# One order for five engines, written by a clock: a state-space and mixture-of-experts layer on Trainium2

## The chip, the cores and the metric

The kernel runs on one core of one Trainium2 chip. A core has TensorE (PE; its weight loads are shown as PEld), VectorE (DVE), ScalarE (ACT), GpSimd (POOL) and SyncE (SP), which here issues every DMA transfer. Each engine takes its instructions strictly in the order in which they are written, and waits for the others by semaphores. The metric is the time of one execution on the device in microseconds (us): 2043.07 is the median of three runs before the change, which lie between 2033.55 and 2044.17.

## The reference

The input is u, 4 sequences of 2048 tokens of 256 numbers, all in float32. The layer has two halves, each with a residual:

```python
x = x + ssm(layernorm(x));   x = x + moe(layernorm(x))
# ssm: x, z = split(u @ W_in.T + b_in);  delta, B, C from x @ W_x.T + b_x
#   delta = softplus(delta_raw @ W_dt.T + b_dt);  A = -exp(A_log)        # 512 x 16
#   for each token: h = h * exp(delta * A) + x * delta * B;  y = sum_n(h * C)
#   (y + x * D) * silu(z) @ W_out.T + b_out
# moe: 4 experts, softmax router, top 2, weights w (not renormalized)
#   h_e = relu(x @ Wi.T + lora_e);  out = sum_e w_e * (h_e @ Wo.T)       # 1024 wide
```

The mean and variance of a layernorm are taken over the 256 numbers of a token; eps is 1e-5.

## The kernel before

**Tiling.** The tokens are cut into 16 chunks of 512 (`TC`), four to a sequence. Inside a chunk the channels lie on the 128 partitions in four blocks (`d`), and time runs along the free axis, so that one `tensor_tensor_scan` on VectorE carries one of the 16 states `n` of one block through 512 tokens. There are 64 scans in a chunk, 1024 in all (the list `states`).

**One state.** `decay(i)` on ScalarE writes exp(delta * A) into one of three PSUM buffers dA. `enter(i)` on GpSimd multiplies delta * x by B for two states at once (dBx). `scan(i)` on VectorE joins the two. `read(i)` multiplies by C: on VectorE into hC, or, for 5 of 16 states (`SHARED`), on GpSimd into hP, in which case the scan writes hS. `sum_y(i)` on TensorE adds the result to y by four transposes. `keep(i)` on ScalarE copies the last column as the carry of the next chunk. B and C are broadcast from DRAM by SyncE (`load_bc`). A decay has to wait until the read three states earlier has freed its buffer.

**Around the states.** `front(c)` makes chunk c's inputs: layernorm, its transpose to xnT, the projections `p_in`, delta with softplus, and the gate with silu. `close_y` copies y, turns it back and gates it; `tail(c)` makes the output projection `po` and adds it to u; `ffn(c)` holds the second layernorm, the router (`p_route` to `mask`) and eight half-tiles k of the expert layer: `p_low` (LoRA of the second-best expert, then the difference to the best one), `p_base`, relu, transpose `p_hT`, copy `a_hT`, and, once for two half-tiles, the down projection `p_down` (pf) with its `add`. The relu of each of the two experts is a ScalarE ACTIVATE with the expert's weight as scale (`a_relu`), and both results are transposed into the same PSUM tile. Only the last chunk (`late`) adds the second relu on VectorE (`d_relu`) and transposes once; it then scales by the best expert's weight in `add`.

**LayerNorm.** `layernorm_T` takes the statistics of four 128-token tiles on VectorE (`bn_stats`, `bn_aggr`), 1/sqrt on GpSimd in four small operations (`rstd`), and applies them with four ScalarE ACTIVATEs (`norm`).

**What sets the order.** Every operation goes through `InOrder`, which fixes each engine's order as the program order. A main loop writes the scans i = 0 to 1023 in turn, with the decay two and dBx four states ahead and `sum_y` two or three states behind. All other work is cut into `Step`s with a rough cost. `Pacer.fill` is called twice for each state and puts in the steps that a rough clock calls ready: for VectorE only with a margin of 0.5 us behind their inputs and for at most 0.8 us at a time (`fits`, `ready`). `force` writes what a deadline asks for. Work that does not fit waits, and `begin(c)`, called when chunk c - 1 closes, adds the next chunk's steps behind it. Three PSUM banks ("mm") are shared by all these steps. The order on every engine is fixed when the program is built.

## Time and profile before

| what | value |
|---|---|
| median of 3 runs | 2043.07 us (2033.55 to 2044.17) |
| profiled execution | span 2037.5 us from its first to its last instruction; the page gives no other total |
| busy VectorE / GpSimd / TensorE / ScalarE | 1818.6 / 1779.0 / 1820.4 / 1424.0 us |
| TENSOR_TENSOR_SCAN, all kinds | 1024, from 31.04 us on |
| mean granted TensorE clock | 0.950 |
| ACT_TABLE_LOAD | 64, 82.1 us |

The page gives, for each engine, the busy time and the number of instructions, then the busy share in 40 equal slices, the chain that ended last, and groups of instructions: line, engine, operation, tile written <- tiles read, shape, count, busy us, mean ns of one, and the idle time before them with what ended it. All operations here go through line 30, the recording helper, so groups are told apart by their tiles: plg is the router, pz the expert pre-activations, h the relu output, phT its transpose, pf the down projection, st and mv the layernorm statistics. Durations of successive instructions on an engine overlap a little; TensorE's ends are modelled.

### The profile page before, as it was taken

The numbers are of one execution on the slowest core, as the hardware profiler recorded it, in microseconds if no ns is written. First come the engines' busy times: TensorE is split into PE (matmuls) and PEld (weight loads), VectorE is DVE, ScalarE is ACT, GpSimd is POOL, SyncE is SP. The second block draws the span as 40 slices with busy tenths as digits, with TensorE's granted clock in tenths as the row PEclk, the third lists the DMA queues.
The fourth block names the chain that finished last, engine by engine and source line by source line (L and its number), as shares of the span: only waits on it lengthen the run. The fifth ranks groups of instructions, "written<-read, shape, count | busy, mean of one in ns | idle before, by whom it ended". The sixth has DMA issues, their size and how long they took to land.

```text
span 2037.5 us, 28634 instructions
## 1 busy us (share of the span) xinstructions
PE 1820.4 (89%) x9472; PEld 1251.9 (61%) x9472; DVE 1818.6 (89%) x2370; ACT 1424.0 (70%) x2890; POOL 1779.0 (87%) x1148
## 2 busy tenths in 40 slices
PE   7577798797998998999889899999999898998899
PEld 4445476566666675766557575666756566575655
DVE  3999999899999999999989899899999999899811
ACT  4677777676777768777686777677696877766432
POOL 4999999898999998999998998899999998999600
PEclk8688899798999999999999999999999999998999
DMA  7444445344445453454535344354544544454200
GB/s 237 151 163 157 143 148 171 130 157 164 158 145 166 149 171 137 159 176 144 182 129 175 133 166 149 126 168 141 178 152 160 164 147 158 135 175 145 74 0 21
DMA packets 106132, 300.70 MB, mean 148 GB/s; under 512 B 12864, under 2 KB 39104, under 8 KB 105984
## 3 DMA queue, kind: packets, MB, share of 16 engines
q1 hardware_dynamic: 105984, 298.88, 43.9%
q8 instruction: 74, 1.21, 0.2%
q14 instruction: 74, 0.61, 0.1%
HBM read 289.41 MB, written 9.44 MB: 147 GB/s over the span
## 4 chain that ended last, share of the span: by engine, by line
PE 29%; DVE 14%; ACT 10%; issue 4%; POOL 1%; DMA 0%; DVEq 0%; POOLq 0%; ACTq 0%
PE pz L30 10%; PE y L30 6%; DVE dA L30 6%; PE pf L30 5%; ACT dA L30 4%; PE pin L30 3%; DVE hS L30 3%; DVE hC L30 3%; PE phT L30 2%; ACT L30 1%; ACT delta L30 1%; ACT g L30 1%; PE po L30 1%; DVE u L30 1%; POOL dBx L30 1%
## 5 line engine op out<-in xcount | busy, mean ns | idle before, releaser
L30 POOL TENSOR_TENSOR dBx<-xdt,B 128x1024 f32<-128x1024 f32 x512 | 1205.7, 2363 | 60.4 <-DVE dA L30 20.6
L30 ACT ACTIVATE dA<-delta,a_sb 128x512 f32<-128x512 f32 x1024 | 708.5, 694 | 144.7 <-DVE hC L30 89.6
L30 DVE TENSOR_TENSOR_SCAN dA<-dA,carry,dBx 128x512 f32<-128x512 f32 x528 | 661.1, 1277 | 38.7 <-ACT dA L30 28.2
L30 DVE TENSOR_TENSOR hC<-dA,C 128x512 f32<-128x512 f32 x704 | 470.8, 669 | 0.0
L30 PE MATMUL y<-ident,hC 128*128 128x128 f32 x2816 | 431.8, 284 | 24.4 <-DVE hC L30 24.3
L30 POOL TENSOR_TENSOR hP<-hS,C 128x512 f32<-128x512 f32 x320 | 408.1, 1275 | 2.8 <-PE y L30 2.4
L30 PEld LDWEIGHTS y<-ident,hC 128*128 128x128 f32 x2816 | 344.2, 147 | 105.3 <-DVE hC L30 39.7
L30 DVE TENSOR_TENSOR_SCAN hS<-dA,carry,dBx 128x512 f32<-128x512 f32 x240 | 305.2, 1272 | 22.3 <-ACT dA L30 17.3
L30 PE MATMUL pin<-xnT,w_in_sb 128*128 128x512 f32 x512 | 252.0, 620 | 23.2 <-ACT dbc L30 5.3
L30 PE MATMUL pz<-wi_sb,x2T 128*128 128x512 f32 x512 | 266.1, 645 | 0.0
L30 PEld LDWEIGHTS y<-ident,hP 128*128 128x128 f32 x1280 | 159.7, 147 | 163.9 <-issue 79.8
L30 ACT COPY carry<-dA 128x1 f32<-128x1 f32 x528 | 82.9, 157 | 241.5 <-DVE hC L30 240.3
L30 PE MATMUL y<-ident,hP 128*128 128x128 f32 x1280 | 205.9, 286 | 50.4 <-POOL hP L30 50.2
L30 PE MATMUL pf<-wo_sb,hT 128*128 128x256 f32 x1024 | 238.6, 381 | 6.8 <-ACT hT L30 3.9
L30 DVE TENSOR_TENSOR_SCAN dA<-dA,dBx 128x512 f32<-128x512 f32 x176 | 209.6, 1219 | 14.8 <-ACT dA L30 11.8
L30 ACT ACTIVATE h<-pz,topv 128x512 f32<-128x512 f32 x248 | 167.1, 679 | 77.4 <-PE pz L30 76.6
L30 PEld LDWEIGHTS pf<-wo_sb,hT 128*128 128x128 f32 x1024 | 187.3, 190 | 35.1 <-ACT hT L30 5.2
L30 PE MATMUL pz<-bm_sb,lowT 16*128 16x512 f32 x512 | 167.7, 650 | 23.8 <-ACT delta L30 6.9
L30 PEld LDWEIGHTS pz<-wi_sb,x2T 128*128 128x128 f32 x512 | 93.0, 202 | 121.0 <-issue 121.0
L30 PEld LDWEIGHTS pin<-xnT,w_in_sb 128*128 128x128 f32 x512 | 92.7, 198 | 116.5 <-issue 80.1
L30 PE MATMUL phT<-ident,h 128*128 128x128 f32 x992 | 132.2, 275 | 6.0 <-ACT delta L30 3.1
L30 PEld LDWEIGHTS phT<-ident,h 128*128 128x128 f32 x992 | 114.6, 142 | 31.3 <-issue 17.4
(99 smaller groups left out, 1786.6 us busy)
## 6 DMA issues: line engine op xcount, KB each, us to landing
B<-bc SPq DMA_DIRECT2D x256, 512.0 KB, 3.7
C<-bc SPq DMA_DIRECT2D x256, 512.0 KB, 3.8
ua<-in_u_dram SPq DMA_DIRECT2D x16, 512.0 KB, 5.3
u<-in_u_dram SPq DMA_DIRECT2D x16, 512.0 KB, 5.4
out_dram<-u SPq DMA_DIRECT2D x16, 512.0 KB, 4.8
w_in_sb<-in_w_inT_dram SPq DMA_DIRECT2D x2, 512.0 KB, 4.7
wi_sb<-in_wiT_dram SPq DMA_DIRECT2D x1, 1024.0 KB, 7.2
wo_sb<-in_woT_dram SPq DMA_DIRECT2D x1, 1024.0 KB, 10.6
```

The source lines that it names most:

```text
L30: return self._tc.keep_in_program_order(f(*args, **kwargs))
```

## The change

The order is no longer written by a loop with fillers. All work, scans and decays too, is made of `Step`s with an occupancy, a tail (time until the result is seen) and a due time, counted in states. `Clock.run` takes, over all five engines, the step that can start first; among those of one engine that could start within `SOON` of each other, the one that is due first. `start` counts data, bank and buffer waits; every buffer's release is given as a dependency. TensorE is written down as 1.095 times slower than its full-rate times (`FAST`). A `veto` keeps other ScalarE work from delaying the next decay, until it is overdue. Chunk c - 1's router is due 14 to 30 states, its expert layer 30 to 80 states after chunk c begins. ACT_TABLE_LOADs are counted in the clock.

Beside this: layernorm's mean and sum of squared deviations are taken by two ScalarE ACTIVATEs per tile with a running sum (`mean`, `spread`), into one junk tile, and `rstd` has three operations; every chunk now does what only the last one did: the second expert's relu, scaled by rho (the second-best expert's exponential), is written by ScalarE, the best expert's relu is added to it on VectorE, there is one set of transposes, and `add` scales by `top0` = 1 / sum of exponentials; the router keeps unnormalized exponentials, whose sum comes from the exponential itself, and saves a sum, a multiplication and a copy on VectorE. SHARED, buffer numbers and the three banks are as before.

```diff
-class Pacer:
-    LATENCY = 0.2
-    MARGIN = 0.5
-    LONG = 1.0
-    MOST = 0.8
-    BEGIN = {"pe": 0.7, "act": 0.6, "pool": 0.5, "sp": 0.0}
-    END = {"pe": 2.2, "act": 1.5, "pool": 2.5, "sp": 99.0}
...
-    def fits(self, x, begin):
...
-    def ready(self, x):
...
+    TAIL = {"pe": 0.18, "act": 0.11, "dve": 0.1, "pool": 0.055, "sp": 4.0}
...
+    WAKE = {"pe": 0.055, "act": 0.037, "dve": 0.06, "pool": 0.08, "sp": 0.1}
+    SOON = {"pe": 0.05, "act": 0.02, "dve": 0.02, "pool": 0.05, "sp": 0.05}
+    TABLE = 1.294
...
+    def start(self, x):
+        t = self.free[x.engine]
+        w = self.WAKE[x.engine]
+        for y in x.after:
+            if y.done is None:
+                return None
+            if y.done + w > t:
+                t = y.done + w
+        if x.locks and self.locked:
+            return None
+        if x.takes:
+            if len(x.takes) > sum(b is not None for b in self.bank):
+                return None
+            t = max(t, sorted(b for b in self.bank if b is not None)[len(x.takes) - 1] + w)
+        return t
+    def write(self, x, t):
+        for k in x.takes:
+            k.at = min((b, n) for n, b in enumerate(self.bank) if b is not None)[1]
+            self.bank[k.at] = None
+        x.begin = t
+        self.free[x.engine] = t + self.occ(x)
+        x.done = self.free[x.engine] + x.tail
+        if x.table:
+            self.table = x.table
+        for k in x.gives:
+            self.bank[k.at] = x.done
+        self.locked = (self.locked or x.locks) and not x.unlocks
+        if x.emit:
+            x.emit()
+        if x.then:
+            x.then()
+    def choose(self, engine):
+        seen = []
+        for thread in self.threads:
+            q = thread.of.get(engine)
+            if q:
+                t = self.start(q[-1])
+                if t is not None:
+                    seen.append((t, q[-1], thread))
+        if not seen:
+            return None
+        if self.strict:
+            seen = [s for s in seen if not self.veto(s[1], s[0])]
+            if not seen:
+                return None
+        soon = min(s[0] for s in seen) + self.SOON[engine]
+        return min((s for s in seen if s[0] <= soon), key=lambda s: (s[1].due, s[0]))
+    def run(self):
+        while self.threads:
+            picks = [p for p in map(self.choose, self.free) if p]
+            if not picks:
+                self.strict = False
+                picks = [p for p in map(self.choose, self.free) if p]
+                self.strict = True
+            assert picks, "nothing can be written"
+            t, x, thread = min(picks, key=lambda p: p[0])
+            thread.of[x.engine].pop()
+            thread.left -= 1
+            if not thread.left:
+                self.threads.remove(thread)
+            self.write(x, t)
...
-        def stats(j):
-            if j == 0:
-                q["mv"] = small.tile([P, NJ, 2], F32, tag=f"mv{name[0]}", name=f"mv_{name}")
-            x = small.tile([P, 6], F32, tag="st", name=f"st_{name}_{j}")
-            dve.bn_stats(x, src()[:, j, :])
-            dve.bn_aggr(q["mv"][:, j, :], x)
+        def mean(j):
+            if j == 0:
+                q["nm"] = small.tile([P, NJ], F32, tag=f"nm{name[0]}", name=f"nm_{name}")
+                q["sq"] = small.tile([P, NJ], F32, tag=f"sq{name[0]}", name=f"sq_{name}")
+            junk = work.tile([P, DM], F32, tag="junk", name=f"jm_{name}_{j}", bufs=1)
+            act.activation(
+                junk, src()[:, j, :], AF.Copy, scale=-1.0 / DM, accum_out=q["nm"][:, j : j + 1]
+            )
+        def spread(j):
+            junk = work.tile([P, DM], F32, tag="junk", name=f"js_{name}_{j}", bufs=1)
+            act.activation(
+                junk, src()[:, j, :], AF.Square, bias=q["nm"][:, j : j + 1], accum_out=q["sq"][:, j : j + 1]
+            )
...
-            pool.tensor_scalar_add(ve, q["mv"][:, :, 1], EPS)
-            pool.tensor_tensor(q["rstd"], ve, mhalf, ALU.pow)
-            pool.tensor_tensor(ve, q["mv"][:, :, 0], q["rstd"], ALU.mult)
-            pool.tensor_scalar_mul(q["nmr"], ve, -1.0)
+            pool.tensor_scalar(ve, q["sq"], 1.0 / DM, EPS, ALU.mult, ALU.add)
+            pool.tensor_tensor(q["rstd"], ve, mhalf, ALU.pow)
+            pool.tensor_tensor(q["nmr"], q["nm"], q["rstd"], ALU.mult)
...
-        steps = [Step("dve", 0.54, lambda j=j: stats(j)) for j in range(NJ)]
+        steps = [Step("act", 0.41, lambda j=j: mean(j)) for j in range(NJ)]
+        steps[0].after = list(ready)
+        steps += [Step("act", 0.45, lambda j=j: spread(j)) for j in range(NJ)]
...
-        def exp_():
-            for j in range(NJ):
-                act.activation(room(1)[:, j, :], room(0)[:, j, :], AF.Exp, bias=q["red"][:, j : j + 1])
-        def softmax():
-            sm = small.tile([P, NJ], F32, tag="sm", name=f"sm_{c}")
-            dve.tensor_reduce(sm, room(1), AX.X, ALU.add)
-            dve.reciprocal(sm, sm)
-            p_ = q["p"] = small.tile([P, NJ, E], F32, tag="p_", name=f"p_{c}")
-            dve.tensor_tensor(p_, room(1), sm[:, :, None].to_broadcast([P, NJ, E]), ALU.mult)
-            dve.tensor_copy(room(2), p_)
+        def exp_():
+            q["sm"] = small.tile([P, NJ], F32, tag="sm", name=f"sm_{c}")
+            q["e"] = small.tile([P, NJ, E], F32, tag="e", name=f"e_{c}")
+            for j in range(NJ):
+                act.activation(
+                    room(1)[:, j, :], room(0)[:, j, :], AF.Exp, bias=q["red"][:, j : j + 1],
+                    accum_out=q["sm"][:, j : j + 1],
+                )
+            act.copy(q["e"], room(1))
+        def softmax():
+            s["top0"] = small.tile([P, NJ], F32, tag="top0", name=f"top0_{c}")
+            dve.reciprocal(s["top0"], q["sm"])
...
-            mp = small.tile([P, TOPK, NJ, E], F32, tag="mp", name=f"mp_{c}")
-            pool.tensor_tensor(mp, m, q["p"][:, None, :, :].to_broadcast([P, TOPK, NJ, E]), ALU.mult)
-            s["topv"] = fold(mp, (P, TOPK, NJ), "topv").rearrange("p k j o -> p k (j o)")
+            me = small.tile([P, NJ, E], F32, tag="me", name=f"me_{c}")
+            pool.tensor_tensor(me, m[:, 1], q["e"], ALU.mult)
+            s["rho"] = fold(me, (P, NJ), "rho").rearrange("p j o -> p (j o)")
...
-        def ratio():
...
-            r = small.tile([P, NJ], F32, tag="sm", name=f"r_{c}")
-            dve.reciprocal(r, s["top0"])
-            dve.tensor_tensor(s["topv"][:, 1, :], s["topv"][:, 1, :], r, ALU.mult)
...
-            q["h", k, 0] = q["h", k, 1]
-            dve.scalar_tensor_tensor(q["h", k, 1], q["z", k], 0.0, q["h", k, 1], ALU.max, ALU.add)
-            h = q["h", k, slot] = scanp.tile([P, HF], F32, tag="hC", name=f"h{slot}_{c}_{k}", bufs=4) if late else work.tile([P, HF], F32, tag=f"h{slot}", name=f"h{slot}_{c}_{k}")
-            act.activation(h, q["z", k], AF.Relu, scale=s["topv"][:, slot, k // 2 : k // 2 + 1])
+            dve.scalar_tensor_tensor(q["h", k], q["z", k], 0.0, q["h", k], ALU.max, ALU.add)
+        def a_relu(k):
+            q["h", k] = work.tile([P, HF], F32, tag=f"h{k % 2}", name=f"h_{c}_{k}", bufs=1)
+            act.activation(q["h", k], q["z", k], AF.Relu, scale=s["rho"][:, k // 2 : k // 2 + 1])
-            for slot in (1,) if late else (1, 0):
-                for b in range(HF // P):
-                    pe.matmul(
-                        pm[:, b * P : (b + 1) * P], lhsT=q["h", k, slot][:, b * P : (b + 1) * P], rhs=ident,
-                        is_transpose=True, start=(slot == 1 and b == 0), stop=late or slot == 0,
+                pe.transpose(pm[:, b * P : (b + 1) * P], q["h", k][:, b * P : (b + 1) * P], ident)
...
-                dve.tensor_tensor(s["u"][:, j, :], q["f", j][:, :DM], s["u"][:, j, :], ALU.add)
...
-                    hs.append(Step("dve", 0.6, lambda k=k: d_relu(k - SK), after=[low, z1s[k - SK]]))
-                else:
-                    hs.append(Step("act", 0.57, lambda k=k: a_relu(k - 1, 0), after=[low], gives=1))
+                hs.append(
+                    Step("dve", 0.6, lambda k=k: d_relu(k - SK), after=[low, z1s[k - SK]],
+                         gives=[] if late else [bank("z", k - SK)])
+                )
...
+                z1s.append(Step("act", 0.57, lambda k=k: a_relu(k), after=[bases[-1], tops] + hTs[k - 2 : k - 1]))
...
+            if i % (NN * ND2) == 0:
+                for h, used in ((0, X), (1, C)):
+                    x = Step("sp", 0.33, lambda ib=ib, h=h: load_bc(ib, h), after=[at["bc", c]], due=i - 9 + 2 * h)
...
+            A[i] = Step("act", 0.623, lambda i=i: decay(i), after=[at["soft", c], *free, *ready], tail=0.07, table="exp", due=i - 0.9)
...
+                X[i] = X[i + 1] = Step("pool", 2.307, lambda i=i: enter(i), after=[at["xdt", c, d], Bl[ib], *free], due=i - 2.0)
...
+            S[i] = Step(
+                "dve", 1.175 if c % CPB else 1.114, lambda i=i, k=k: scan(i, k),
+                after=[A[i], X[i], *free, *([K[i - PER]] if i - PER in K else [])], due=i,
...
+                C[i] = Step("pool", 1.222, lambda i=i, k=k: read(i, k), after=[S[i], Cl[ib], *free], due=i + 1.5)
...
+        S[c * PER + PER - AHEAD].then = lambda: begin(c + 1)
+    AHEAD = 12
...
+        if c:
+            t = tail(c - 1)
+            clock.add(t, (o + DUE["tail"][0], o + DUE["tail"][1]))
+            norm, route, inner = ffn(c - 1, [t[-1]])
+            clock.add(norm + route, (o + DUE["route"][0], o + DUE["route"][1]))
+            clock.add(inner, (o + DUE["inner"][0], o + DUE["inner"][1]))
...
+    DUE = {
+        "front": (-4, 46), "gate": (14, 54), "silu": 10, "tail": (3, 14), "route": (14, 30), "inner": (30, 80),
+    }
+    SPARE = 0.1
...
+        latest = v - 0.76 - SPARE
+        end = t + clock.occ(x) + (clock.TABLE if x.table not in (None, "exp") else 0)
+        lead = clock.start(A[nexts])
+        if lead is None:
+            lead = clock.free["dve"] + 0.75
+        if end <= max(latest, lead + 0.02):
+            return False
+        now = next((i for i in range(max(nexts - 4, 0), M) if S[i].done is None), M)
+        return x.due + 2 > now if x.occ < 1.5 else x.due > now
...
-    for i in range(M + 4):
-        pacer.quiet = (i + 5) % (PER // NH) < 8
...
-            S[i] = pacer.run("dve", 1.2 if states[i][0] % CPB else 1.14, lambda: scan(i), [A[i], X[i]])
-        if i + AHEAD_B < M and i % NN == 0:
-            X[i + AHEAD_B] = X[i + AHEAD_B + 1] = pacer.run(
-                "pool", 2.32, lambda: enter(i + AHEAD_B), [S[i - 1]]
-            )
-        pacer.fill()
...
+    begin(0)
+    clock.run()
```

## The prediction

> **What bounds the kernel now.** I read the page's head and slices, then busy time by stages, then what VectorE waited for between the first and the last scan, then the last 110 us by the order of time, then single rows for prices.
>
> ```profile
> span 2037.5 us, 28634 instructions
> PE 1820.4 (89%) x9472; PEld 1251.9 (61%) x9472; DVE 1818.6 (89%) x2370; ACT 1424.0 (70%) x2890; POOL 1779.0 (87%) x1148
> ...
> PEclk8688899798999999999999999999999999998999
> ```
>
> Three engines share the load, so the average says little. The first scan starts at 31.0 us, the last read by VectorE ends at 1926.1. By stages (columns: length, then busy us of PE, PEld, DVE, ACT, POOL, then granted clock, DMA share, GB/s):
>
> ```profile
> 31.00:1926.10 1895.10, 1693.71 (x8984) 1176.23 (x8985) 1797.29 (x2311) 1378.92 (x2816) 1769.40 (x1121) 0.95 0.46 154
> 1926.10:2037.50 111.40, 104.97 (x430) 63.92 (x428) 16.89 (x44) 30.90 (x54) 3.10 (x10) 0.97 0.03 10
> 810.00:935.00 125.00, 120.64 (x660) 84.47 (x660) 121.81 (x163) 98.02 (x179) 119.85 (x78) 1.00 0.47 156
> 1185.00:1310.00 125.00, 115.50 (x592) 79.50 (x590) 114.47 (x147) 90.07 (x197) 111.42 (x71) 0.93 0.45 148
> 1560.00:1685.00 125.00, 117.97 (x643) 82.05 (x642) 121.69 (x158) 96.42 (x211) 118.59 (x75) 1.00 0.49 161
> ```
>
> While scans run, VectorE sets the pace: 1797.3 busy, 97.8 idle of 1895.1. Where the granted clock was 1.00 its idle time was 3.2 and 3.3 us in 125; at 0.93 it was 10.5. So about half of the 97.8 (3.25/125 of 1895 is 49) comes with the written order, and the other half with TensorE at half rate. What it waited for in that stage:
>
> ```profile
> DVE dA L30 <- ACT dA L30: 40.0, 77, 3.7
> DVE hS L30 <- ACT dA L30: 21.2, 26, 2.9
> DVE hS L30 <- ACT carry L30: 7.2, 8, 2.7
> ...
> DVE g L30 <- PE py L30: 0.7, 1, 0.7
> DVE u L30 <- PE po L30: 0.5, 1, 0.5
> ```
>
> (Columns: us in total, times, longest.) 61 us is a decay that ScalarE made late; TensorE held VectorE directly for 1.2 us only. The last stage is TensorE's (105.0 busy of 111.4), because it does two FFNs: VectorE takes chunk 14's router at 1919 us, chunk 15's at 1964.
>
> ```profile
> 1919.23 0.15 DVE L30 TENSOR_TENSOR plg<-plg,bg_sb 128x16 f32<-128x16 f32 x1
> ...
> 1964.15 0.18 DVE L30 TENSOR_TENSOR plg<-plg,bg_sb 128x16 f32<-128x16 f32 x1 [8.41 <-ACT low L30]
> ```
>
> **The tail.** In the new instruction order, chunk 14's router stands 38 scans before the end, 6 of its 8 relu-adds before the last scan, and two of its four down projections too. Behind the last y transposes stand, against before: 48 down matmuls for 64, 40 h transposes for 96, 18 base for 32, 17 low for 32. At the start-to-start times of this tail (0.43, 0.22, 0.91 and 0.53 us) that is 6.9 + 12.2 + 12.8 + 8.0 = 39.9 us of TensorE moved beside the scans. The tail doesn't shrink by all of it, since chunk 15's chain then stands uncovered. From the last read: gate 5 us; po 7.3 with 4.1 of chunk 14 between (16.4); add 0.7; LayerNorm statistics on ScalarE, 8 at about 0.55 (21.5); rstd on GpSimd and four norms 4.0 (25.5); turn and copy 2.9 as before (28.4); router, softmax and mask 9, which took 11.3 before with TensorE busy elsewhere (37.4). From chunk 15's first low matmul (1973.1) to the last down matmul (2033.3) were 60.2 us, with 15 of chunk 14 inside (two bases 3.6, two downs 7.0, two lows 2.1, transposes 2.2), so 45 (82.4); the last add and store 4.2, as from 2033.3 to the end. Tail about 87 for 111.4: minus 24. Bounds: minus 40 if the chain overlaps, minus 10 if the inner part keeps its 60 us. The two ends of that part are these rows of TensorE:
>
> ```profile
> 1973.08 1.98 PE L30 MATMUL pz<-bm_sb,lowT 16*128 16x512 f32 x6
> ...
> 2029.70 3.62 PE L30 MATMUL pf<-wo_sb,hT 128*128 128x256 f32 x16
> ```
>
> **VectorE beside the scans.** Out: 120 bn_stats with bn_aggr, 0.585 each: 70 us; three softmax steps x15 (0.154 + 0.174 + 0.178): 7.6. In: 118 relu-adds at the 0.692 of the eight that the tail already has: 82; 58 fused adds, 0.484 for 0.405: 4.6. Sum plus 8.
>
> ```profile
> L30 DVE SCALAR_TENSOR_TENSOR h<-pz,h 128x512 f32<-128x512 f32 x8 | 5.5, 692 | 20.7 <-PE pz L30 20.7
> L30 ACT ACTIVATE h<-pz,topv 128x512 f32<-128x512 f32 x248 | 167.1, 679 | 77.4 <-PE pz L30 76.6
> L30 ACT ACTIVATE xn_f<-u,nmr_f,rstd_f 128x256 f32<-128x256 f32 x64 | 36.7, 593 | 1.9 <-POOL nmr_f L30 1.7
> ```
>
> So relu for relu the swap wins nothing. The Trainium skill, "ScalarE: Activation LUTs", Rules for kernel authors, says to use VectorE and not ScalarE for relu and add, up to about 3x faster in bf16. In this float32 case the rows say 692 against 679 ns; by the page's factor the 82 us would be about 27, and the sum below 55 us lower.
>
> **ScalarE.** In: 248 statistics beside the scans, 256 wide, with a sum taken. No row has one; below, the norm's issue distance 0.49, above, 0.593 and then a wait on the one before (they share a junk tile): 0.65. Between 122 and 161 us; I take 0.55, 136, nearest the same-width norm. Out: 112 relus at 0.679, 76. With chunk 14's work, ScalarE goes from 1379 to about 1450 of 1875. It is covered while a decay is ready; table loads stay at 64. The new statistics wait for u's last add or the ua transfer, and behind them on ScalarE stand decays, so a late transfer now holds ScalarE where it held VectorE (4.1 us once, at 36.4 us).
>
> **GpSimd and SyncE.** GpSimd loses the 30 scalings (0.241), and about 2 us of router: 1769 to 1760, hidden. SyncE issues the same 618 instructions. The store and the u, ua loads move against the B and C loads; GpSimd waited 0.6 us for B in all, landings are 3.7 us, the new order asks about 8 scans (14 us) early. Zero; with one B load per chunk late by a store's 4.8 us it would be 16 x 4.8 = 77.
>
> **TensorE.** 480 transposes less at 0.109 start to start: 52 us, of which 49 beside the scans; chunk 14's 40 comes in. Minus 9 on 1694, no bound. The granted clock was 0.80 from 65 to 185 us, mostly chunk 0 with no FFN yet, and 0.95 over all scans. The Trainium skill, "TensorE: Matmul & The Clock Gate", Part 4, says transposes don't count as busy for the clock; taken so, fewer of them leave the 0.95 as it is, and no term here changes.
>
> **Prologue.** The first statistics take 8 x 0.55 on ScalarE for 2.2 on VectorE, and GpSimd gives 0.24 back; TensorE waits for its other work till 12.6 anyway. First scan plus 1: 32.
>
> **Idle time of VectorE.** This is the unknown. The order is written with the occupancies that the trace shows (decay 0.623, scan 1.175, dBx 2.307) and a TensorE 9.5% slow, so the half that comes with half rate (49) I halve to 25; the half that is the order's (49) I lower by the 4 of the ua wait: 45. Idle 70. Bounds: 40 (no clock part) and 98 plus 60, that is 118 relu-adds each waiting 0.5 us for TensorE: 158. I take 70 since 3.2 per 125 was reached in two whole windows.
>
> **Sum.** 32 + 1805 + 70 + 87 = 1994 of span, against 31.0 + 1797.3 + 97.8 + 111.4 = 2037.5. The page has no total of its execution beside the span; the median 2043.1 lies 5.6 above it, the three runs reach from 2033.6 to 2044.2. I add 5.6: 2000.
>
> **Rivals.** (1) The order does better: idle 45, tail 84: 1966 + 5.6 = 1972. For it, windows at clock 1.00; against, ScalarE's added 70 us. (2) The order doesn't do what it says: idle stays 98, only the tail is won: 2022 + 5.6 = 2028. For it, softplus and silu still block ScalarE for 1.28 + 1.91 + 1.28, and three decay buffers remain. (3) Slower: relu-adds on VectorE wait for TensorE. They are written as soon as TensorE should be done, so every half-rate stretch (after 185 us the records hold 67 us of lost clock) lands on VectorE, and scans queue behind. Break-even is idle 113; at 0.5 us for each of 118 relu-adds on top of today's 98, 2088. Against it: the order plans TensorE slow. (4) TensorE becomes the bound: its 100 us a chunk (64 y sums, projections and FFN at the trace's full-rate start-to-start times, 103 before less 3.5 of transposes) would be 125 at the 0.80 that 65 to 185 us had; sixteen times 125 with prologue and tail is 2125. Only if the start's clock stayed.
>
> **How the numbers follow.** Forecast 0.44 (own range 1982 to 2018); (1) 0.20; (2) 0.16, mostly below 2033; (3) 0.16; (4) 0.04. 0.5%, 10 us, is about what a measurement can tell from no change. Faster (below 2033): 0.44 + 0.20 + 0.10 = 0.74; same: 0.06 of (2) and 0.03 of (3), 0.09; slower: 0.17. The range 1948 to 2062 leaves out about 0.06 below (idle near 40 with the tail bound of minus 40) and 0.13 above.
>
> **What would show it.** Right: bn_stats gone, VectorE beside the scans near 1805 busy and 70 idle, "DVE h <- PE pz" below 15 us there, router 15 as the only one behind the last scan, tail 82 to 92. Wrong: VectorE waits on PE pz or on ACT dA above 60 us each; granted clock below 0.9; POOL dBx waits for DMA B.

## The result, and the profile after

The changed kernel takes 2059.42 us (median of 4 runs, 2058.6 to 2062.0) against 2041.42 (4 runs, 2033.55 to 2044.17): 1.009 times as long, 95% interval 1.0061 to 1.0119. The forecast was 2000 us and, with a chance of 0.74, a faster kernel. The time lies inside the stated range, which ended at 2062; the sign is wrong.

The page of the changed kernel:

```profile
span 2057.5 us, 27962 instructions
...
PE 1853.3 (90%) x8992; PEld 1226.6 (60%) x8992; DVE 1818.1 (88%) x2183; ACT 1488.4 (72%) x3362; POOL 1769.0 (86%) x1116
...
PEclk8868899999999989999899999999899998998979
```

By stages, cut as in the prediction (length, busy us of PE, PEld, DVE, ACT, POOL, granted clock, DMA share, GB/s):

```profile
32.70:1964.00 1931.30, 1751.57 (x8641) 1165.34 (x8639) 1801.11 (x2146) 1446.80 (x3272) 1760.11 (x1091) 0.93 0.44 151
1964.00:2057.50 93.50, 76.27 (x284) 47.55 (x282) 14.64 (x31) 21.92 (x53) 2.75 (x9) 0.86 0.03 12
```

| us of the profiled execution | before | forecast | after |
|---|---|---|---|
| up to the first scan | 31.0 | 32 | 32.7 |
| VectorE busy beside the scans | 1797.3 | 1805 | 1801.1 |
| VectorE idle there | 97.8 | 70 | 130.2 |
| tail | 111.4 | 87 | 93.5 |
| span | 2037.5 | 1994 | 2057.5 |

Three terms came out as worked out or nearly so. The idle time went up by 32 us where it was to fall by 28; that one term is 60 of the 63.5 us by which the span was missed. What VectorE waited for in that stage (us in total, times, longest):

```profile
DVE dA L30 <- ACT dA L30: 45.3, 53, 3.8
DVE dA L30 <- POOL dBx L30: 38.1, 18, 3.0
DVE g L30 <- PE py L30: 21.1, 19, 2.3
DVE hS L30 <- ACT dA L30: 9.9, 6, 2.4
DVE h L30 <- PE pz L30: 8.7, 14, 2.9
DVE hS L30 <- ACT xT L30: 4.2, 1, 4.2
DVE hS L30 <- POOL dBx L30: 1.1, 1, 1.1
```

By these rows late decays cost 55 us, for 61 before, and dBx 39 for 3. But a row names, of all that an instruction waits for, whatever signalled last before it started, and that need not be what it needed. Scan 10 of chunk 5 in after:

```profile
645.45 2.36 POOL L30 TENSOR_TENSOR dBx<-xdt,B 128x1024 f32<-128x1024 f32 x1 [0.47 <-DVE dA L30]
...
653.87 2.35 POOL L30 TENSOR_TENSOR dBx<-xdt,B 128x1024 f32<-128x1024 f32 x1
...
655.50 1.30 ACT L30 ACTIVATE dA<-delta,a_sb 128x512 f32<-128x512 f32 x2
...
656.28 1.29 DVE L30 TENSOR_TENSOR_SCAN dA<-dA,carry,dBx 128x512 f32<-128x512 f32 x1 [2.91 <-POOL dBx L30]
```

This scan reads the dBx that began at 645.45 and had been ready for 8.5 us; the one that ends just before it is for scans 14 and 15. Its decay, the first of the two from 655.50 on, ended 0.09 us before it, so the wait is the decay's. Sorted in this way for every scan, by the ends of the decay and the dBx that it reads, late decays cost 87 us (80 before) and dBx 7 (0.3 before); py, the transposed y that the gate waits for, costs 21 (0.7 before) and pz 9 (none before). The 32 us are thus 7 of decays, 20 of py, 9 of pz and 7 of dBx, less some 10 of short gaps and a DMA wait that are gone. The largest piece of the decays' 87 is the 41 us at scan 10.

Two more readings come from the trace's records, summed by the place of the scan in its chunk (0 to 63). VectorE's idle time lies at scan 10 (41 us over 14 chunks), at scans 32 to 40 (44 us), at 55 and 56 (14) and at 1 (8). And TensorE was granted half rate for 288 us in all, 206 before; of that, 133 us are stretches that begin in scans 48 to 63 of chunks 1 to 15, where it was 48 before. Two of these places in after, scans 48 to 63 of chunks 7 and 8, the first with half rate and the second without:

```profile
968.00:999.00 31.00, 26.31 (x114) 17.10 (x114) 28.46 (x34) 18.12 (x39) 27.43 (x16) 0.80 0.40 136
1090.00:1117.00 27.00, 22.70 (x119) 14.13 (x117) 27.00 (x33) 20.11 (x55) 25.83 (x14) 1.00 0.45 156
```

In both TensorE has a lull (busy 0.85 and 0.84 of the time; before, these scans have 0.97 and 0.98). Where the lull brought half rate (0.80), VectorE stood idle 2.5 us and the stretch took 4 us more than the other (the remaining 1.5 are VectorE's own work). Part of the way there goes through ScalarE: at 981.9 us a relu waited 2.8 us for pz, the decay stood behind it on ScalarE, and scan 55 waited 1.9 us for that decay.

### The profile page after: what moved, and what is told of

Its sections match the earlier page's. It is cut to its first block, busy times and chain, and to the rows that moved or that the text cites. A ratio compares the mean times of both kernels' runs of the same rounds, so it can differ in the third digit from the quotient of the medians.

```text
span 2057.5 us, 27962 instructions
## 1 busy us (share of the span) xinstructions
PE 1853.3 (90%) x8992; PEld 1226.6 (60%) x8992; DVE 1818.1 (88%) x2183; ACT 1488.4 (72%) x3362; POOL 1769.0 (86%) x1116
## 5 line engine op out<-in xcount | busy, mean ns | idle before, releaser
L30 ACT ACTIVATE dA<-delta,a_sb 128x512 f32<-128x512 f32 x1024 | 683.8, 686 | 102.1 <-DVE hC L30 94.9
L30 PE MATMUL y<-ident,hC 128*128 128x128 f32 x2816 | 450.8, 291 | 81.6 <-DVE hC L30 79.4
L30 PE MATMUL pz<-wi_sb,x2T 128*128 128x512 f32 x512 | 270.9, 656 | 0.0
L30 PEld LDWEIGHTS y<-ident,hP 128*128 128x128 f32 x1280 | 155.4, 146 | 135.1 <-POOL hP L30 85.8
L30 PEld LDWEIGHTS pf<-wo_sb,hT 128*128 128x128 f32 x1024 | 185.4, 190 | 21.6 <-issue 1.4
L30 PE MATMUL pz<-bm_sb,lowT 16*128 16x512 f32 x512 | 190.3, 709 | 5.1 <-ACT hT L30 2.5
L30 PEld LDWEIGHTS pz<-wi_sb,x2T 128*128 128x128 f32 x512 | 98.9, 215 | 93.5 <-issue 93.5
L30 ACT ACTIVATE h<-pz,rho 128x512 f32<-128x512 f32 x128 | 86.8, 678 | 83.1 <-PE pz L30 62.0
L30 PE MATMUL po<-w_out_sb,g 128*128 128x256 f32 x512 | 123.8, 385 | 3.1 <-DVE u L30 2.4
L30 DVE SCALAR_TENSOR_TENSOR h<-pz,h 128x512 f32<-128x512 f32 x128 | 86.8, 678 | 37.1 <-PE pz L30 36.9
```

The source lines that it names most:

```text
L30: return self._tc.keep_in_program_order(f(*args, **kwargs))
```

## Experiments

What each run measured, in one table. Each ratio is to before as measured beside that run. The columns from "first scan" on are from the profiled execution, cut as above; it was the longest of ten runs for run 13 (2057 us) and the shortest for runs 3 (2045) and 8 (2021). Half rate is the time during which the clock records show it.

| kernel | median us | ratio to before, 95% | first scan | VectorE busy | idle | tail | half rate |
|---|---|---|---|---|---|---|---|
| before | 2041.4 | | 31.0 | 1797.3 | 97.8 | 111.4 | 206 |
| after | 2059.4 | 1.009 (1.0061 to 1.0119) | 32.7 | 1801.1 | 130.2 | 93.5 | 288 |
| 1 new operations, old order | 2131.6 | 1.045 (1.0429 to 1.0471) | 31.1 | 1802.4 | 185.4 | 113.9 | 434 |
| 2 old statistics and relus, new order | 2031.1 | 0.9946 (0.9925 to 0.9966) | 33.5 | 1783.7 | 123.6 | 88.5 | 206 |
| 3 later wake-up from TensorE | 2053.4 | 1.0063 (1.0043 to 1.0083) | 34.9 | 1803.3 | 108.6 | 96.8 | 244 |
| 4 idle matmuls | 2031.7 | 0.9953 (0.9931 to 0.9974) | 32.5 | 1796.9 | 106.3 | 94.6 | 131 |
| 5 idle transposes | 2031.5 | 0.9944 (0.9922 to 0.9967) | 32.8 | 1798.9 | 103.5 | 94.4 | 125 |
| 6 relus on ScalarE | 1981.2 | 0.9698 (0.9681 to 0.9715) | 32.6 | 1732.1 | 127.1 | 88.2 | 148 |
| 7 statistics on VectorE | 2101.4 | 1.0286 (1.0266 to 1.0307) | 33.7 | 1854.6 | 122.3 | 91.5 | 357 |
| 8 idle matmuls, xdt spread | 2026.1 | 0.9914 (0.9892 to 0.9937) | 32.4 | 1799.2 | 92.9 | 94.5 | 121 |
| 9 silu due later | 2111.1 | 1.035 (1.0315 to 1.0386) | 33.1 | 1805.8 | 174.6 | 94.8 | 394 |
| 10 relus on ScalarE, idle matmuls | 2053.9 | 1.0094 (1.0061 to 1.0127) | 33.1 | 1736.8 | 183.8 | 97.2 | 142 |
| 11 relus on ScalarE, xdt spread | 2000.9 | 0.9801 (0.9776 to 0.9827) | 32.8 | 1733.2 | 140.1 | 91.5 | 182 |
| 12 no silu loads | 2056.7 | 1.0072 (1.0048 to 1.0095) | 34.5 | 1804.2 | 124.9 | 94.9 | 306 |
| 13 no softplus loads | 2043.3 | 1.0024 (0.9995 to 1.0054) | 32.3 | 1802.6 | 124.2 | 96.5 | 319 |
| 14 neither | 2027.9 | 0.9927 (0.9901 to 0.9953) | 34.0 | 1801.7 | 97.6 | 94.9 | 251 |
| 15 neither, idle matmuls | 2001.8 | 0.9811 (0.9793 to 0.9828) | 33.0 | 1799.4 | 72.9 | 94.8 | 111 |
| 16 neither, relus on ScalarE | 1960.3 | 0.9609 (0.9591 to 0.9627) | 33.1 | 1735.9 | 102.9 | 88.2 | 169 |

### Is it the order or the operations? (runs 1, 2, 6, 7)

Run 1 puts the new operations into before's loop and pacer (statistics, relus, router, `add`); run 2 leaves the new order and takes the statistics and the best expert's relus back, with the edits shown below for runs 7 and 6 together (the smaller router and the scaled `add` stay).

```diff
 # run 1, in before.  In front: the statistics
-        steps = [Step("dve", 0.54, lambda j=j: stats(j)) for j in range(NJ)]
+        steps = [Step("act", 0.53, lambda j=j: mean(j)) for j in range(NJ)]
+        steps += [Step("act", 0.62, lambda j=j: spread(j)) for j in range(NJ)]
...
 # in ffn: every chunk as only the last one did
-                    hs.append(Step("act", 0.57, lambda k=k: a_relu(k - 1, 0), after=[low], gives=1))
+                hs.append(Step("dve", 0.6, lambda k=k: d_relu(k - SK), after=[low, z1s[k - SK]], gives=int(not late)))
```

> The kernel before with its own order (the main loop and the rough clock), and only the operations changed: LayerNorm statistics on ScalarE, the second relu added by VectorE, one set of transposes, the smaller router. Theory A (the new order costs the time, the operations are neutral): VectorE's busy time beside the scans rises by 5 to 10 us, the kernel takes 2025 to 2050 us. Theory B (the operations cost it: ScalarE has 70 us more to do ahead of the decays, and VectorE waits for TensorE before its 118 relu-adds): 2055 us or more, with VectorE's waits for ACT dA well above 61 us or for PE pz above 20 us.

> The changed kernel with its order by the clock, but LayerNorm statistics back on VectorE and both relus back on ScalarE with two sets of transposes (the smaller router stays). Theory A: stays near the changed kernel, 2050 to 2080 us, the last stage again short (about 93 us), and idle time of VectorE beside the scans again above 110 us. Theory B: 2000 to 2040 us, idle below 90 us.

Runs 6 and 7 take back one of the two alone:

```diff
 # run 6: the best expert's relu on ScalarE, two sets of transposes
-            dve.scalar_tensor_tensor(q["h", k], q["z", k], 0.0, q["h", k], ALU.max, ALU.add)
+            if late: ...                       # chunk 15 as before
+            act.activation(q["h0", k], q["z", k], AF.Relu)
...
 # run 7: the statistics on VectorE
-        steps = [Step("act", 0.41, lambda j=j: mean(j)) for j in range(NJ)]
-        steps += [Step("act", 0.45, lambda j=j: spread(j)) for j in range(NJ)]
+        steps = [Step("dve", 0.525, lambda j=j: stats(j)) for j in range(NJ)]
```

> The changed kernel with the relus alone undone: both on ScalarE, two sets of transposes; LayerNorm statistics stay on ScalarE (into the tile that the norm writes next). VectorE loses about 80 us of work, ScalarE gains 80, TensorE 50. Theory A2 (the fewer transposes open the lull): half-rate time about 205 us, 2015 to 2040 us. Theory B2 (ScalarE's load is what delays the decays): ACT dA waits above 75 us and the time at 2050 or more.

> The changed kernel with the LayerNorm statistics alone back on VectorE. VectorE's busy time beside the scans goes from 1801 to about 1865. If VectorE's load sets the pace, 2085 to 2125 us; if ScalarE's load does (Theory B2), the decays come earlier, ACT dA falls from 55 to below 35 us, and the time stays below 2065.

The stage beside the scans of runs 1, 2, 6 and 7:

```profile
31.10:2018.90 1987.80, 1731.13 (x8567) 1172.12 (x8567) 1802.44 (x2140) 1439.61 (x3265) 1761.99 (x1090) 0.90 0.44 147
```

```profile
33.50:1940.80 1907.30, 1762.46 (x9107) 1188.01 (x9107) 1783.65 (x2260) 1400.72 (x2908) 1767.91 (x1116) 0.95 0.46 153
```

```profile
32.60:1891.80 1859.20, 1725.50 (x9112) 1176.78 (x9111) 1732.13 (x2028) 1494.56 (x3389) 1759.27 (x1090) 0.97 0.46 157
```

```profile
33.70:2010.60 1976.90, 1770.67 (x8640) 1177.81 (x8639) 1854.57 (x2378) 1343.34 (x2790) 1768.91 (x1116) 0.92 0.43 148
```

Read the third column of busy times, VectorE, and the length before it. Under the new order, in runs 2, 6, 7 and after, the idle time is 122 to 130 us whatever the operations are, and the time follows VectorE's busy time. So the change falls into three parts, each measured by a pair. The order with the old statistics and relus: 2038.7 (before, beside run 2) to 2031.1, minus 8; its tail is 23 us shorter, its idle time 26 longer and VectorE's busy time 14 shorter, part of it by the smaller router. The statistics on ScalarE: minus 50 (run 2 to run 6) or minus 42 (run 7 to after). The relu-adds on VectorE: plus 78 (run 6 to after), of which 69 are VectorE's busy time and 5 the tail, or plus 70 (run 2 to run 7). Minus 8, minus 50 and plus 78 make plus 20, and so do minus 8, plus 70 and minus 42. Run 1 shows that the new operations gain nothing under the old order either: there they cost 93 us, with 185 idle.

Of the expectations, run 1 fits Theory B (2131.6 us, decays 92 by the rows, though pz only 4), and run 7 the first one (2101.4). Run 2 has the time of Theory B with the idle time of Theory A. Run 6 was below both of its ranges.

The same pairs tell of the clock. With one set of h transposes in place of two, half rate went from 148 to 288 us (run 6, after) and from 206 to 357 (run 2, run 7). The relu-adds on VectorE change with them, and stretch the time over which TensorE has its work, so this alone does not tell which of the two lowered the clock.

### The clock (runs 3, 4, 5, 10)

Run 3 gives a TensorE result 0.5 us more before another engine may count on it (`TAIL`, pe: 0.18 to 0.68). Run 4 puts seven matmuls of 512 columns, whose results nobody reads, into scans 49 to 61 of each chunk, where the lull is; run 5 puts eight transposes in each of those places.

```diff
+            if i % PER in (49, 51, 53, 55, 57, 59, 61):
+                bd = Bank()
+                def warm(bd=bd, i=i):
+                    pe.matmul(mm_tile(bd, f"warm_{i}"), lhsT=w_in_sb[:, 0, :P], rhs=w_in_sb[:, 0, :TC], start=True, stop=True)
+                clock.add([Step("pe", FULL, warm, after=[S[i]], takes=[bd], gives=[bd], tail=0.18, due=i + 2.4)])
```

> The changed kernel with one number changed: the time from the end of TensorE's work to its result, as the clock counts it, 0.68 us for 0.18. Theory A1 (the order has no margin for a late TensorE): VectorE's waits for PE py and PE pz beside the scans, 30 us together, fall below 12 us, and the time falls to 2030 to 2048 us. Rival: the later placing only moves the loss to the decays (ACT dA above 65 us), and the time stays within 5 us of 2059 or rises.

> The changed kernel with 7 idle matmuls of 512 columns in each chunk, one after every second scan from the 49th to the 61st, whose results nobody reads. Theory A2 (the order leaves TensorE short of work in the last quarter of a chunk, where 133 of its 190 us at half rate fall, and its lateness behind that costs VectorE time): half-rate time falls below 100 us, the waits for PE py from 21 to below 10, time 2035 to 2052 us. Rival (half rate there is harmless, TensorE has slack): half-rate time falls but the time stays within 5 us, or rises by up to 10 as y comes later.

> As the run with idle matmuls, but in each of the 7 places eight idle transposes of 128 columns, 0.87 us, in place of one matmul of 0.86. Theory A2a (any TensorE work in the lull keeps the clock): half-rate time about 131 us as with the matmuls, 2025 to 2040 us. Theory A2b (transposes don't count as activity, as the skill's TensorE page says): half-rate time stays above 220 us and the time at 2050 to 2070.

In run 4 the same two stretches as above, scans 48 to 63 of chunks 7 and 8, and the whole stage:

```profile
954.00:982.00 28.00, 26.16 (x122) 15.30 (x120) 28.00 (x33) 17.49 (x37) 26.76 (x15) 1.00 0.46 151
1072.00:1099.00 27.00, 25.96 (x123) 15.81 (x123) 27.00 (x33) 19.10 (x53) 25.97 (x14) 1.00 0.49 156
...
32.50:1935.70 1903.20, 1767.70 (x8858) 1156.72 (x8856) 1796.91 (x2146) 1448.53 (x3270) 1759.73 (x1090) 0.97 0.46 154
```

And the stage of run 5:

```profile
32.80:1935.20 1902.40, 1766.06 (x9527) 1216.87 (x9526) 1798.87 (x2146) 1447.35 (x3269) 1760.55 (x1090) 0.98 0.45 154
```

The clock is 1.00 in both stretches and 0.97 to 0.98 over the stage for 0.93; the idle time at scans 55, 56 and 1 fell from 22 us to 0.1, and the kernel is 28 us faster with more work in it. Transposes did the same as matmuls: half rate 125 and 131 us, medians 2031.5 and 2031.7. Run 4 went beyond its theory in time (2031.7 for 2035 to 2052) with more half rate left than it asked for (131 us for below 100); run 5 went as Theory A2a said. Run 3 did little, 6 us, and fits neither side: the py wait stayed (22.8 us for 21.1), the pz wait rose (11.4 for 8.7), and the decays' did not rise.

One rival stays untested. All three edits make the clock write the order anew, and in run 3, with no idle work at all, the half rate that begins in scans 48 to 63 fell from 133 to 55 us as well (7 and 0 in runs 4 and 5). No run gave the idle step its place in the order without its instructions. That the gain of 24 and 27 us of idle time comes from the clock rests on where it lies: 22 of it are at the scans that the lulls held up.

Run 10 puts run 4's matmuls into run 6.

> The version with the relus on ScalarE (1981 us) with the same seven idle matmuls per chunk at scans 49 to 61. Theory: they gain where TensorE falls to half rate in that place, and here it doesn't (0 us of half rate in scans 40 to 64 of the chunks, against 133 in the changed kernel); so nothing is gained, idle time of VectorE 122 to 132, median 1977 to 1986. Rival: the idle matmuls help by something else than the clock there (they shift the written order, or pace TensorE): a gain like the 28 us that they brought in the changed kernel, median 1950 to 1960.

```profile
33.10:1953.70 1920.60, 1794.36 (x9315) 1212.11 (x9314) 1736.79 (x2028) 1499.40 (x3386) 1762.63 (x1090) 0.97 0.45 152
```

Both expectations missed. Nothing was gained, as the theory said, since there was no half rate in that place to lose (outside chunk 0); but it cost 73 us. VectorE's idle time rose by 57 us, 55 of it at scans 16 to 21; in the whole stage late decays cost 107 us for 90, and waits for y rose from 1 to 28. Why just there wasn't found. An edit to one place is felt elsewhere, as the clock writes all that follows anew.

### GpSimd's burst and ScalarE's blocks (runs 8, 9, 11)

In after, the four xdt products of the next chunk stand close together on GpSimd (scans 35 to 44; in 5 of 15 chunks in one burst of 4.95 us), and the rows give 39 us of waits for dBx, so the burst was taken for their cause. It is not: sorted by what each scan reads, dBx is late for 7 us in all, nearly all of it at scans 2 to 14, and the other 32 are late decays, nearly all at scan 10. Runs 8 and 11, expected on that ground, spread the products over scans 47 to 57 of the chunk before; run 9 moves the due time of the silu from scan 10 to 28 (`"silu": 10` to `28`).

```diff
             at["xdt", c, m] = xdts[m]
+            if c and m:
+                xdts[m].after.append(S[(c - 1) * PER + 42 + 5 * m])
```

> The run with idle matmuls, and in addition the four products delta * x of the next chunk, which GpSimd does in a burst behind softplus, held back so that one stands after every fifth scan or so. Theory D (the burst makes dBx late): VectorE's waits for POOL dBx fall from 31 to below 10 us and the time from 2031.7 to 2005 to 2020. Rival (what is late there is ScalarE's softplus block, and dBx only comes last): ACT dA rises by as much as POOL dBx falls, and the time stays within 5 us.

> The changed kernel with the due time of the silu block (table load 1.28, silu 1.91, table load 1.28 us on ScalarE) moved from scan 10 of a chunk to scan 28. VectorE now stands idle about 2.9 us at scan 10 of 14 chunks, 41 us in all. Theory: the block takes 4.5 us of ScalarE in one piece, more than the decays made ahead can bridge, wherever it stands; the idle time moves to the new place and stays within 120 to 138 us, median 2050 to 2068. Rival: scan 10 is a bad place, where the gates and the router's work want ScalarE as well; then most of the 41 us go, idle time 90 to 100, median 2020 to 2030.

> The version with the relus on ScalarE with the four xdt products of GpSimd spread over scans 47 to 57 of the chunk before, where they stand in one burst now (4.95 us). VectorE waits 15 us for dBx there, and about 48 us of half rate stand in scans 32 to 40. Theory: the burst holds up dBx and through it the y sums; spread, 6 to 13 us are won: idle time 114 to 121, median 1968 to 1975. Rival: with the relus ScalarE is the next in line (1495 us busy of 1859), and what dBx gives back the decays take: idle time stays at 124 to 130, median 1978 to 1984.

Run 8 is 5.6 us faster than run 4, less than its theory asked; the idle time at scan 10 fell from 36 to 14 us, and the waits for dBx, sorted as above, stayed (9 us for 7). On run 6's operations the same edit cost 20 us (run 11), with 19 us of idle time at scan 4 for 3 there. Run 9 moved the idle time of scan 10 (41 us to 0.6) to scans 28 and 29 (34 us), and in scans 32 to 37 there were 79 us for 28, with half rate grown to 394 us. None of the three came out as either side expected. What they teach is the scatter: a small edit that rewrites the order moved the idle time by minus 13 (run 8), plus 13 (run 11), plus 44 (run 9) and plus 57 us (run 10). So runs with the order untouched had to decide.

### The order kept, loads taken away (runs 12 to 16)

Silu and softplus each stand on ScalarE between two table loads. In after, around scan 10 of chunk 7:

```profile
893.89 1.28 ACT L30 ACT_TABLE_LOAD   x1
...
895.18 1.91 ACT L30 ACTIVATE g<-g 128x2048 f32<-128x2048 f32 x1
...
897.11 1.28 ACT L30 ACT_TABLE_LOAD   x1
...
898.40 1.30 ACT L30 ACTIVATE dA<-delta,a_sb 128x512 f32<-128x512 f32 x2
...
899.20 1.29 DVE L30 TENSOR_TENSOR_SCAN dA<-dA,carry,dBx 128x512 f32<-128x512 f32 x1 [2.73 <-ACT dA L30]
```

Nothing of the decays comes for 4.5 us, and the scan stands still for 2.73. Runs 12 to 14 take the loads away by another function. They compute other values and serve to measure alone; every engine keeps its order, instruction by instruction.

```diff
-            act.activation(s["g"], s["g"], AF.Silu)
+            act.activation(s["g"], s["g"], AF.Identity)        # runs 12, 14, 15, 16
-            act.activation(s["delta"], s["delta"], AF.Softplus)
+            act.activation(s["delta"], s["delta"], AF.Exp)     # runs 13, 14, 15, 16
```

> The changed kernel, its instruction order kept as it is on every engine, with the silu replaced by a plain copy (the gate is left unactivated), so that ScalarE's block is 1.91 us in place of 1.28 + 1.91 + 1.28. Theory: the 41 us for which VectorE stands idle at scan 10 of the chunks are the two table loads; idle time 130 falls to 85 to 98, median 2018 to 2030. Rival: the order would be held up there anyway (a late py or z, TensorE at half rate), and the idle time appears some scans later: idle 115 to 130, median 2045 to 2060.

> The changed kernel, its instruction order kept, with the softplus of delta replaced by an exp (other values, the same shapes), which is the decays' own table: the block on ScalarE is 1.9 us in place of 1.28 + 1.91 + 1.28. VectorE stands idle 44 us in scans 32 to 40 of the chunks. Theory: the softplus block makes the decays and what follows late there; idle time 130 falls to 95 to 110, median 2025 to 2040. Rival: that place waits for the burst of four xdt products on GpSimd and for y sums at half rate, which the block only precedes: idle 120 to 132, median 2048 to 2062.

> Both of the last two edits together, instruction order kept. Theory: the two blocks are the order's own half of the idle time and the half rate the rest, so the two gains add: idle 60 to 80 and median 1985 to 2010. Rival: without them TensorE or GpSimd is next in line, the gains don't add, idle 90 to 115, median 2020 to 2045.

Run 12, waits of VectorE beside the scans:

```profile
DVE dA L30 <- ACT dA L30: 40.4, 56, 3.8
DVE h L30 <- PE pz L30: 33.7, 28, 2.9
```

and the same place, scan 10 of chunk 7, in order of time:

```profile
899.93 0.49 DVE L30 SCALAR_TENSOR_TENSOR u<-pf,top,u 128x256 f32<-128x256 f32 x1
...
900.47 1.99 PE L30 MATMUL po<-w_out_sb,g 128*128 128x256 f32 x8 [0.24 <-DVE u L30]
...
902.83 1.12 PE L30 MATMUL pz<-bm_sb,lowT 16*128 16x512 f32 x2
...
903.99 0.69 DVE L30 SCALAR_TENSOR_TENSOR h<-pz,h 128x512 f32<-128x512 f32 x1 [2.38 <-PE pz L30]
```

The loads are gone and 31 of the 41 us at scan 10 are still there, 24 of them now in front of a relu-add. Its z stands on TensorE behind 2 us of output projection, which starts only after an add on VectorE (0.24 us of waiting). In after this second wait lay under the first: a scan held up by its decay gave z the time to come. Over the whole stage late decays fell from 87 to 59 us, and waits for pz rose from 9 to 34. So the rival held for run 12: what was taken from ScalarE, a relu-add lost to TensorE at the same scan. Run 13's median lies between its two expectations, with single runs from 2031 to 2057 us. Both edits together win 31.6 us, more than the 19 of the two alone; idle 97.6 and 2027.9 us lie in the rival's range (less than the theory's sum).

Runs 15 and 16 make both edits in run 4 and run 6.

> The version with seven idle matmuls per chunk (2031.7 us, VectorE idle 106 us) with silu replaced by a copy and softplus by an exp (other values), instruction order kept. Theory: half rate (24 us, already gone here) and the two blocks with table loads make up what the idle time lies above the forecast of 70, and TensorE's lateness behind the silu (relu-adds that waited 1.7 us at scan 10 once the loads were gone) came from half rate; idle time 60 to 75, median 1988 to 2003. Rival: the relu-adds at scan 10 wait for TensorE by the written order, at full rate too, so the blocks' loss is only handed over: idle 84 to 100, median 2010 to 2028.

> The version with the relus on ScalarE (1981 us, VectorE idle 127 us) with the same two replacements, instruction order kept. Here no relu-add stands on VectorE beside the scans, so nothing of VectorE waits for z. Theory: the blocks' loss isn't handed over to a relu-add, and the gain is larger than the 31 us of the changed kernel: idle 75 to 92, median 1930 to 1946. Rival: y sums, GpSimd or the decays themselves take over; gain of 31 or less, idle 96 to 125, median 1950 to 1979.

Run 15, the stage and the longest waits of VectorE in it:

```profile
33.00:1905.30 1872.30, 1744.94 (x8857) 1151.73 (x8855) 1799.36 (x2146) 1364.96 (x3208) 1759.35 (x1090) 0.98 0.46 156
```

```profile
DVE h L30 <- PE pz L30: 24.4, 17, 2.8
DVE g L30 <- PE py L30: 10.7, 8, 2.1
DVE dA L30 <- ACT dA L30: 10.5, 21, 1.5
```

With half rate and loads both gone, the idle time is 72.9 us and the time 2001.8, within the theory's ranges, and close to the 70 and 2000 that were forecast for the kernel with both losses in it. The theory's other half fell: at a clock of 0.98 the relu-adds still wait 24 us for pz, so that wait is written into the order. In run 16 the theory fell and the rival's ranges held: with no relu-add beside the scans the loads are worth 21 us, not more than 31. What takes over there (33 to 37 scans into the chunk, 38 us, of it 15 py and 17 decays) was not followed up.

## Why the prediction was wrong

**The step that failed** is "Idle 70". It halved "the half that comes with half rate (49)" to 25 and lowered "the half that is the order's (49)" to 45. The first half came out near its size, as far as the runs tell: runs 4 and 5, with the lulls' half rate gone, have 24 and 27 us less idle time (what the 131 and 125 us of half rate that they keep cost is not known). The second did not: what remains is 104 to 106 us, not 45, and it is there without the new relus and statistics too (run 2: 124 idle, at the clock of 0.95 that before had with 98). Of it, 33 are the table loads of silu and softplus (run 14 against after, run 15 against run 4); the rest of about 73 is, in run 15 and sorted by what each scan reads, relu-adds behind pz (24), decays (16), py (11), dBx (11), and smaller waits. "I take 70 since 3.2 per 125 was reached in two whole windows" carried a figure of the old order over to an order that had not run. The prediction's rival (2) said itself that the blocks of 1.28 + 1.91 + 1.28 remain; they had been given no price in the forecast. Its bounds, 40 and 158, held. One reading ahead of it was short as well: the 61 us of late decays before are 80 of the 97.8 when each scan is held against the decay that it reads: late decays held most of the idle time from the start.

**The clock.** "Taken so, fewer of them leave the 0.95 as it is, and no term here changes" was worked out from Part 4 of the Trainium skill's page "TensorE: Matmul & The Clock Gate", by which transposes don't count as busy. Run 5 speaks against that in this kernel, as far as its rewritten order allows: with eight idle transposes per place the clock was as high as with a matmul (0.98 and 0.97). In the two pairs above half rate nearly doubled with the 480 transposes gone (148 to 288, 206 to 357 us); that they were the activity that is missing is argued, since the relu-adds moved with them. The measurement decides here; the page's transposes may be of another kind than these float32 ones, which no run here tells.

**VectorE.** "Sum plus 8" is measured as plus 3.8; a relu-add took 0.678 us (forecast 0.692). "So relu for relu the swap wins nothing" was right, and it was the sentence to go on with. Beside the scans a microsecond of work on VectorE cost about a microsecond of the kernel (69 of the 78 us of run 6 against after), while one on ScalarE, busy for 1447 of 1931 us, cost little: run 6 has 48 us more on ScalarE than after, and its late decays cost 90 us for 87. The prediction summed the two swaps to plus 8, and didn't ask which of them to make: the 70 us that the statistics freed on VectorE were spent on relu-adds for 82.

**ScalarE, GpSimd, SyncE, prologue.** Forecast about 1450, 1760, 0 and 32; measured 1446.8, 1760.1, beside the scans no wait for a load above 2.2 us, and 32.7. A statistic took, from start to start of two in a row, 0.54 us (mean) and 0.62 (deviations), and 0.41 and 0.51 in front of a decay, for the 0.55 taken; the accumulating ACTIVATE is short, but each is followed by a second instruction:

```profile
L30 ACT ACTIVATE js_a<-ua,nm_a 128x256 f32<-128x256 f32 x64 | 32.4, 506 | 0.8
...
L30 ACT ACTIVATE jm_a<-ua 128x256 f32<-128x256 f32 x64 | 26.5, 414 | 3.5 <-DMA ua<-in_u_dram 2.5
...
L30 ACT ACTIVATION_READ_ACCUMULATOR js_a<-ua,nm_a 128x1 f32 x64 | 12.1, 189 | 0.0
...
L30 ACT ACTIVATION_READ_ACCUMULATOR jm_a<-ua 128x1 f32 x64 | 12.1, 188 | 0.0
```

"It is covered while a decay is ready" held for these, and not for the silu, behind which a decay is not ready.

**Tail.** Forecast 87, bounds 71 and 101; measured 93.5, with router 15 alone behind the last scan as foreseen. The chain of chunk 15 stands uncovered, with a clock of 0.86 there for 0.97 before: 26 us of it passed at half rate, about 13 lost. In runs 2, 6 and 16 it was 88, with 17 to 23 us at half rate.

**Rivals.** Rival (3) had the sign and its "break-even is idle 113" holds: 130.2 less 113 is 17, and with 6.5 of the tail and the small terms that gives the 20 us by which the span grew. Its mechanism showed only when uncovered, 8.7 us of waits on pz in after and 33.7 in run 12, and not by half rate, which it gave as the reason: at a clock of 0.98 (run 15) they still are 24.4. Rival (2), "only the tail is won", is what the order alone did in net (run 2: minus 8, forecast 2028, measured 2031), though its idle time rose by 26 us, more than the tail's 23, and VectorE's smaller busy time made up for it.

**What would show it.** Of the signs listed for a right forecast, 70 idle and a tail of 82 to 92 failed (130.2 and 93.5). Of those for a wrong one none lit by the rows (pz 8.7 and dA 55 us, each below 60; a clock of 0.93, not below 0.9; 2.2 us of dBx waiting for B). The threshold on decays could not tell: sorted by what each scan reads, they are 87 us in after and 80 before. The idle time as a whole, against the 113 of break-even, would have caught it.

## What to carry to other kernels

Where one engine sets the pace in all stages, price each swap of work by that engine's busy time alone and take each by itself: here one part of the change was worth 42 to 50 us, another cost 70 to 78, and the kernel with the first and without the second (run 6, 1981.2 us, ratio 0.9698, 0.9681 to 0.9715) is faster than both before and after. Do not carry the idle time of one written order over to another; take it from a run, since small edits to this list moved it by up to 57 us. And where an idle stretch has one named releaser, hold the instruction against the ends of what it reads, since the name can be wrong (32 of the 39 us put down to dBx here), and look for the second wait that lies under the first before pricing the first.

## What was not expected of the hardware

TensorE's granted clock fell to half rate in lulls of 0.84 to 0.85 busy, in some chunks and not in others, and work that nobody reads, put into the lulls, made the kernel 28 us faster (ratio to before 0.9953 for 1.009). Transposes of float32 did this as well as matmuls did; the order was written anew with either. Where that place had no half rate (run 10) the same edit cost 73 us, by waits elsewhere in the order. And an ACTIVATE with a running sum is followed by a read of the accumulator of 0.19 us, 320 times in this kernel: 60 us of ScalarE.
